# Last stage of a six-layer perceiver kernel: attention of all four tiles ahead of the ternary layers

## The chip, the cores and the metric

The kernel runs on one core of one Trainium2 chip, as one program. The metric is device microseconds of one execution of the whole program, lower is better. Before the change three executions took 3087.1, 3088.03 and 3089.5 us; the median is 3088.03 us.

## The reference

x holds 8 batches of 64 tokens of width 512, all float32. Six residual layers follow each other; the change lies in the last two, the fifth and sixth, which the kernel computes in one stage:

```python
x = x + _L1_attn_ref(_layernorm(x, axis=-1), Wq, Wk, Wv, u, v, Wo, bo)
x = x + _L1_ffn_ref(_layernorm(x, axis=-1), w1, b1, w2, b2)

# fifth: attention with relative positions, 16 heads of 32, per batch of 64 tokens
scores = (Q @ K.T + u @ K.T + rel_shift(Q @ r.T + v @ r.T)) / sqrt(32)
out = softmax(scores) @ V;  return out @ Wo + bo

# sixth: two ternary linear layers, 512 -> 2048 -> 512
def act_quant(x):                      # levels of -128 to 127 per token
    scale = 127.0 / clip(max(abs(x)), 1e-5)
    return clip(round(x * scale), -128, 127) / scale
def bitlinear(x, w, b):
    return act_quant(rmsnorm(x)) @ weight_quant(w).T + b     # weights of -1, 0, 1
h = gelu(bitlinear(x, w1, b1));  return bitlinear(h, w2, b2)
```

## The kernel before, in words

The 512 tokens are four tiles of 128 tokens (NT = 4, two batches in a tile); x stays in SBUF for the whole program. Five earlier stages run from 0 to about 2900 us of the span and are the same in both kernels. The last stage is `l1_tail` (L1938 to L2262). It works as follows.

- `Group(...).turn` (L1997) normalizes a group's tiles and transposes them (`xt_ps`, L2003); `queries` (L2012) projects them (`q_ps`, L2008) into qu and qv; `keys` (L2092, `k_ps`) and `values` (L2099, `v_ps` L2103) give kT and v. `first` holds tiles 0 to 2; `last` holds tile 3 alone, whose x comes last from the stage before.
- `positions_of(t)` (L2050) computes the relative-position scores `y_ps`, copies them to y and writes them to a DRAM buffer `shift` (L2056); `shifted(t)` (L2065) reads them back displaced as z (L2068). Both DMAs stand in SP's queue, together with the loads of weights (`w1q` L1912, `w2q` L1917) and of the wide biases b1 and b2 (L1971).
- `probabilities(t)` (L2109): sixteen score matmuls `s_ps` (L2041), addition of z (L2115), maximum (L2119), subtraction (L2120), Exp on ScalarE (L2121), sum, reciprocal and product (L2122 to L2124). Apart from the matmuls and the Exp this is on VectorE.
- `turn` (L2127) transposes p on TensorE (`pT_ps`, L2133) with copies on ScalarE (L2134); `attend` (L2137) multiplies by v (`o_ps`, L2146) and selects heads into oT (L2155 on ScalarE, L2156 on VectorE); `out` (L2161) is four matmuls with Wo (`out_ps`, L2164) and the addition to x (L2171).
- `hidden(t)` (L2183): statistics of x (L2188 to L2193), the level through `rms_levels` (L1920; its power of -1/2 is on GpSimd, L57), the rounding (L1933), the transposition `turn_levels` (`levels_ps` L2177, copy L2181), sixteen bf16 matmuls `h_ps` (L2204), then four times: bias and scale (L2208, VectorE), Gelu (L2209, ScalarE), Square with a sum (L2211, ScalarE), maximum (L2212, VectorE). It ends with the addition of b2 to x on GpSimd (L2213).
- `hidden_levels` (L2216) makes the second quantization of the 2048 hidden values; `layer2` (L2225) transposes them (L2177, copies L2179 and L2181), multiplies by w2 (`o_ps`, L2231), adds (L2233) and writes the tile out (L2234).

The code gives an order of calls, and the tile layer's scheduler then interleaves instructions of neighbouring calls on each engine; what each engine executes is the fixed order of the built program. Buffers also bind the order: the PSUM pool `pm` has three banks (tag "mm": s, pT, o, out, o2), `pe` three (tag "e": q, k, y, h), `pt` two (levels); the SBUF tag "ring" has three buffers for qv, p and pT, and "big" has three, which the weights Wq, Wk, Wv hold first and the hidden rows h of the tiles afterwards.

The order of calls before the change: keys, p(0), values, out(0); p(1); all projections of tile 3; then for each t: hidden(t), layer2(t-1), p(t+2), hidden_levels(t), out(t+2), with out(1) in place of layer2 in the first turn. So one tile's ternary layers lie between the attention of two others.

Of the kernel before, what the change touches and what calls it, by code (L numbers as in the profile page):

```python
# [22 lines left out]
NT = B * S // P  # L23
# [1914 lines left out]
def l1_tail(K, x, d, w, known):  # L1938
# [7 lines left out]
    FIRST = NT - 1  # L1946
    with ExitStack() as es:
        ep = es.enter_context(tc.tile_pool(name="e_e", bufs=1, reuse_waits="tile"))
        wp = es.enter_context(tc.tile_pool(name="e_w", bufs=1, reuse_waits="tile"))
# [3 lines left out]
        pm = es.enter_context(tc.tile_pool(name="e_psm", bufs=3, space=PSUM))  # L1953
# [12 lines left out]
        def bank(name):  # L1966
            return pe.tile([P, D], F32, tag="e", name=name)
# [20 lines left out]
        class Group:  # L1988
# [8 lines left out]
            def turn(self):  # L1997
                for i, t in enumerate(self.tiles):
                    xn = ep.tile([P, D], F32, tag="xn", name="xn")
                    K.normalizer(rp, x[:, t : t + 1, :], known[t] if t < FIRST else None)(0, xn)  # L2000
                    ps = bank("xt_ps")
                    for c in range(DC):
                        nc.tensor.transpose(ps[:, ts(c, P)], xn[:, ts(c, P)], K.ident)  # L2003
                    nc.scalar.copy(self.xT[:, :, ts(i, P)], ps.rearrange("p (c n) -> p c n", n=P))
# [45 lines left out]
        def positions_of(t, qv):  # L2050
            y = ep.tile([P, 2, DC, 2, S + 1], F32, tag="y", name="y", bufs=2)
            halves = of_pairs(pe, "e", qv, lambda r, c, b: rT[r], "y_ps")
            nc.gpsimd.memset(y[:, :, :, :, 0:1], 0.0)
            for j in range(2):
                K.copy(y[:, j, :, :, 1:], halves[j])
            nc.sync.dma_start(  # L2056
                shift[t].rearrange("g (p k) -> p g k", k=S + 1), y.rearrange("p j c b k -> p (j c b) k")
            )

        first = Group(ep, list(range(FIRST)))  # L2060
# [27 lines left out]
        groups = [first]  # L2088
# [3 lines left out]
        def keys(g, psum, tag):  # L2092
            n = len(g.tiles) * P
            for c in range(DC):
                ps = psum.tile([P, D], F32, tag=tag, name="k_ps")[:, :n]
                g.project(wk, c, ps)
                nc.scalar.copy(kT[:, c, ds(g.tiles[0] * P, n)], ps)

        def values(g, psum, tag):  # L2099
            for i, t in enumerate(g.tiles):  # L2100
                ps = psum.tile([P, D], F32, tag=tag, name="v_ps")
                for c in range(DC):
                    nc.tensor.matmul(  # L2103
                        ps, lhsT=g.xT[:, c, ts(i, P)], rhs=wv[:, c, :], start=c == 0, stop=c == DC - 1
                    )
                K.copy(v[:, t, :], ps)
                nc.gpsimd.tensor_add(x[:, t, :], x[:, t, :], bo)

        def probabilities(t):  # L2109

            p = ring("j", "p")
            qu = groups[t // FIRST].qu[:, :, t % FIRST]
            halves = of_pairs(pm, "mm", qu, lambda r, c, b: kT[r, c, ds((2 * t + b) * S, S)], "s_ps")
            for j in range(2):
                nc.vector.tensor_add(p[:, j], halves[j], z[t][:, j])  # L2115
            rows = p.rearrange("p j c b k -> p (j c b) k")
            m = rp.tile([P, 16], F32, tag="m", name="m")
            wide = m.unsqueeze(2).to_broadcast([P, 16, S])
            nc.vector.tensor_reduce(m, rows, AX.X, ALU.max)  # L2119
            nc.vector.tensor_sub(rows, rows, wide)  # L2120
            nc.scalar.activation(rows, rows, AF.Exp)  # L2121
            nc.vector.tensor_reduce(m, rows, AX.X, ALU.add)  # L2122
            nc.vector.reciprocal(m, m)
            nc.vector.tensor_mul(rows, rows, wide)  # L2124
            return p
# [11 lines left out]
        def attend(t, pT):  # L2137
            o = [
                pm.tile([P, D], F32, tag="mm", name="o_ps").rearrange("p (c h q) -> p c h q", c=DC, h=2)
                for _ in range(2)  # L2140
            ]
            for c in range(DC):
                for j in range(2):
                    for b in range(2):
                        r = ds(64 * b, 64)
                        nc.tensor.matmul(  # L2146
                            o[b][ds(64 * j, 64), c].rearrange("p h q -> p (h q)"),
                            lhsT=v[r, t, ds(c * P + 64 * j, 64)],
                            rhs=pT[r, j, c, :],
                            start=True,  # L2150
                            stop=True,
                        )
            oT = rp.tile([P, DC, 2, S], F32, tag="oT", name="oT")
            for b in range(2):
                nc.scalar.activation(oT[:, :, b, :], o[b][:, :, 0, :], AF.Copy, scale=own[:, 2:3])  # L2155
                nc.vector.scalar_tensor_tensor(  # L2156
                    oT[:, :, b, :], o[b][:, :, 1, :], own[:, 3:4], oT[:, :, b, :], ALU.mult, ALU.add
                )
            return oT

        def out(t, oT):  # L2161
            ps = pm.tile([P, D], F32, tag="mm", name="out_ps")
            for c in range(DC):
                nc.tensor.matmul(  # L2164
                    ps,
                    lhsT=oT[:, c].rearrange("p b q -> p (b q)"),
                    rhs=wo[:, c, :],
                    start=c == 0,
                    stop=c == DC - 1,
                )  # L2170
            nc.vector.tensor_add(x[:, t, :], x[:, t, :], ps)  # L2171
# [11 lines left out]
        def hidden(t):  # L2183
            y = rp.tile([P, D], F32, tag="y", name="y")
            st = rp.tile([P, 6], F32, tag="lt_st", name="lt_st")
            mv = rp.tile([P, 2], F32, tag="l1_mv", name="l1_mv")
            top = rp.tile([P, 1], F32, tag="top", name="top")
            nc.vector.bn_stats(st, x[:, t, :])  # L2188
            nc.vector.bn_aggr(mv, st)


            nc.vector.tensor_scalar(y, x[:, t, :], mv[:, 0:1], None, ALU.subtract)
            nc.vector.tensor_reduce(top, y, AX.X, ALU.max, apply_absolute_value=True)  # L2193
            level = rms_levels(K, rp, y, top, mv[:, 1:2], 1.0 + EPS, EPS * EPS)
            nc.vector.tensor_mul(level, level, w.size[:, 0:1])
            xT = rp.tile([P, DC, P], BF16, tag="xT", name="xT")
            turn_levels(y, xT, False)
            h = big("h")
            tops = rp.tile([P, 4], F32, tag="tops", name="tops")
            squares = rp.tile([P, 4], F32, tag="squares", name="squares")  # L2200
            for n in range(4):
                ps = bank("h_ps")
                for c in range(DC):
                    nc.tensor.matmul(  # L2204
                        ps, lhsT=xT[:, c, :], rhs=w.w1[:, c, ts(n, 512)], start=c == 0, stop=c == DC - 1
                    )
                hn = h[:, ts(n, 512)]
                nc.vector.scalar_tensor_tensor(hn, ps, level, b1[:, ts(n, 512)], ALU.mult, ALU.add)  # L2208
                nc.scalar.activation(hn, hn, AF.Gelu)  # L2209
                sq = rp.tile([P, D], F32, tag="sq", name="sq")  # L2210
                nc.scalar.activation(sq, hn, AF.Square, accum_out=squares[:, n : n + 1])  # L2211
                nc.vector.tensor_reduce(tops[:, n : n + 1], hn, AX.X, ALU.max, apply_absolute_value=True)  # L2212
            nc.gpsimd.tensor_add(x[:, t, :], x[:, t, :], b2)  # L2213
            return h, tops, squares
# [10 lines left out]
        def layer2(t, h, level):  # L2225
# [7 lines left out]
            nc.vector.scalar_tensor_tensor(o, ps, level, x[:, t, :], ALU.mult, ALU.add)  # L2233
            nc.sync.dma_start(d["out"][ts(t, P), :], o)  # L2234

        keys(first, pm, "mm")
        p = probabilities(0)
        values(first, pm, "mm")
        out(0, attend(0, turn(p)))
        p = probabilities(1)  # L2240
        last = Group(wp, [FIRST])
        last.turn()
        last.queries()
        keys(last, pe, "e")
        values(last, pe, "e")
        positions_of(FIRST, last.qv[0])
        groups.append(last)
        got = None
        for t in range(NT):
            h = hidden(t)  # L2250
            if t == 0:
                out(1, attend(1, turn(p)))
                shifted(FIRST)
            else:
                layer2(t - 1, *got)
            if t + 2 < NT:
                p = probabilities(t + 2)
            got = hidden_levels(*h)
            if t + 2 < NT:
                out(t + 2, attend(t + 2, turn(p)))  # L2260
        layer2(NT - 1, *got)


def program(tc, d):
# [137 lines left out]
```

## Time and profile before

| what | value |
|---|---|
| median of three runs | 3088.03 us |
| the profiled execution's own time | 3083.06 us |
| its span, first to last instruction | 3081.1 us |
| mean granted TensorE clock | 0.987 of full |
| PE, DVE, ACT, POOL busy over the span | 97%, 59%, 27%, 32% |
| from 2944 to 3078 us (134 us): PE, DVE, ACT, POOL busy | 102.3, 88.4, 51.3, 10.3 us |
| granted clock in that stretch | 0.90 |
| last VectorE instruction of the kernel ends (3077.36 + 0.75) | 3078.1 us |

PE is TensorE's matmuls, PEld its weight loads, DVE VectorE, ACT ScalarE, POOL GpSimd, SP the engine whose queue issues the DMAs. A tile is named by what an instruction writes and reads (`out_ps<-L1a_Wo,oT`), L2164 is the line of the kernel. A float32 matmul appears as two records in the profile (x8 for the four matmuls of `out`), a bf16 one as one.

### The profile page before, as it was taken

The page shows a single profiled execution, that of the slowest core. Times are in us where ns is not written, and L with a number is a line of the kernel's source. Part 1 is how long each engine was busy: PE and PEld are TensorE (multiplying, and loading weights), DVE is VectorE, ACT ScalarE, POOL GpSimd, SP SyncE. Part 2 cuts the span into 40 slices and gives each one's busy share as a digit, 9 for nine tenths or more (in the row PEclk, how much of TensorE's full clock was granted, in tenths as well). Part 3 has the DMA queues.
Part 4 walks back from the last instruction along what each step waited for, and adds up shares of the span by engine and source line. Part 5 has one row for each costly group of instructions (what it writes and reads, how often), then busy time and mean ns, then how long its engine had stood idle before and what let it go on. Part 6 is the DMA issues. An engine that isn't in the chain of part 4 may idle for free.

```text
span 3081.1 us, 41104 instructions
## 1 busy us (share of the span) xinstructions
PE 2980.5 (97%) x15515; PEld 2288.4 (74%) x15521; DVE 1830.5 (59%) x3124; ACT 845.5 (27%) x1620; POOL 993.0 (32%) x959
## 2 busy tenths in 40 slices
PE   8999999999999989999999999999999999999887
PEld 7777778888888767888654446778788888888654
DVE  4845545666656656666433333578676676676746
ACT  2322241222222322222111222232332333323234
POOL 4434343544454534444110003221422413304000
PEclk9999999999999999999999999999999999999998
DMA  8265474434434564432659974302112022020260
GB/s 263 71 200 152 145 244 128 140 100 143 131 103 132 180 188 134 128 119 66 228 185 339 343 253 144 92 15 75 42 51 77 21 73 58 22 89 3 87 107 14
DMA packets 387187, 391.76 MB, mean 127 GB/s; under 512 B 55054, under 2 KB 289558, under 8 KB 385838
## 3 DMA queue, kind: packets, MB, share of 16 engines
q1 hardware_dynamic: 380761, 371.80, 39.2%
q10 hardware_dynamic: 5589, 15.24, 1.3%
q8 instruction: 123, 2.02, 0.3%
q0 software_dynamic: 640, 2.10, 0.2%
q14 instruction: 74, 0.61, 0.1%
HBM read 332.90 MB, written 56.16 MB: 126 GB/s over the span
## 4 chain that ended last, share of the span: by engine, by line
PE 58%; DVE 2%; ACT 1%; DMA 1%; issue 0%; POOL 0%; POOLq 0%; ACTq 0%; DVEq 0%; SPq 0%
PE x_ps L1528 11%; PE y_ps L1528 8%; PE s_ps L1691 6%; PE oe_ps L1231 4%; PE h_ps L1204 4%; PE acc L1742 3%; PE x_ps L585 3%; PE x_ps L468 2%; PE z_ps L585 2%; PE z_ps L468 1%; PE sum_ps L1575 1%; PE y_ps L585 1%; PE y_ps L468 1%; DMA wo<-in_L1x_Wp 1%; PE vt_ps L1619 1%; PE top_ps L1727 1%
## 5 line engine op out<-in xcount | busy, mean ns | idle before, releaser
L1588 POOL TENSOR_TENSOR r<-r,minus_half 128x52 f32<-128x52 f32 x32 | 276.9, 8673 | 558.0 <-DVE r L1587 558.0
L468 PE MATMUL x_ps<-qt,ctxT 128*128 128x256 f32 x1152 | 288.1, 384 | 9.6 <-ACT u L428 6.9
L585 PE MATMUL x_ps<-pt,ctx 128*128 128x256 f32 x1152 | 281.7, 382 | 7.2 <-DVE a L561 6.3
L468 PEld LDWEIGHTS x_ps<-qt,ctxT 128*128 128x128 f32 x1152 | 218.7, 192 | 50.4 <-ACT u L428 8.8
L585 PEld LDWEIGHTS x_ps<-pt,ctx 128*128 128x128 f32 x1152 | 217.3, 190 | 41.1 <-DVE a L561 6.5
L136 POOL TENSOR_TENSOR ctxT<-ctxT 128x256 f32<-128x256 f32 x96 | 79.0, 823 | 412.4 <-DMA ctxT<-in_ctxT 284.5
L1691 PE MATMUL s_ps<-qb,kT 128*128 128x256 f32 x832 | 201.2, 381 | 0.1
L449 DVE TENSOR_TENSOR m<-m,s 128x512 f32<-128x512 f32 x176 | 137.5, 781 | 95.8 <-ACT s L447 93.2
L136 POOL TENSOR_TENSOR ctx<-ctx 128x256 f32<-128x256 f32 x96 | 73.5, 765 | 348.5 <-DMA ctx<-in_ctx 275.4
L1691 PEld LDWEIGHTS s_ps<-qb,kT 128*128 128x128 f32 x832 | 154.2, 190 | 26.2 <-issue 3.5
L501 DVE TENSOR_TENSOR s<-s,top_ps 128x1024 f32<-128x1024 f32 (+1 forms) x112 | 123.2, 1135 | 23.3 <-PE top_ps L491 23.3
L1733 DVE TENSOR_TENSOR s<-s,top_ps 128x1792 f32<-128x1792 f32 x64 | 117.9, 1884 | 28.8 <-PE top_ps L1727 28.8
L433 DVE SCALAR_TENSOR_TENSOR s<-y_ps,bias,p 128x256 f32<-128x256 f32 x96 | 46.3, 483 | 146.2 <-PE y_ps L468 145.8
L1701 DVE TENSOR_TENSOR s<-s_ps,r 128x512 f32<-128x512 f32 x192 | 126.4, 682 | 10.8 <-PE s_ps L1691 10.2
L1734 ACT ACTIVATE s<-s 128x1792 f32<-128x1792 f32 x64 | 101.0, 1591 | 84.0 <-DVE s L1733 84.0
L1742 PEld LDWEIGHTS acc<-s,v 128*64 128x64 f32 x1664 | 96.1, 138 | 32.4 <-issue 27.0
L502 ACT ACTIVATE s<-s 128x1024 f32<-128x1024 f32 (+1 forms) x112 | 110.8, 996 | 30.0 <-DVE s L501 25.9
L1742 PE MATMUL acc<-s,v 128*64 128x128 f32 x1664 | 114.9, 280 | 4.1 <-ACT s L1734 4.1
L1204 PE MATMUL h_ps<-w,tok 128*128 128x512 f32 x256 | 117.3, 593 | 0.0
L1231 PE MATMUL oe_ps<-w,hT 128*128 128x512 f32 x256 | 115.6, 593 | 0.0
L515 DVE TENSOR_TENSOR total<-total,s 128x512 f32<-128x512 f32 x160 | 110.0, 687 | 3.5
L468 PE MATMUL x_ps<-qk,ctxT 128*128 128x256 f32 x384 | 104.9, 391 | 6.2 <-ACT s L447 4.0
(472 smaller groups left out, 6287.2 us busy)
## 6 DMA issues: line engine op xcount, KB each, us to landing
w<-in_L0f_W SPq DMA_DIRECT2D x64, 1024.0 KB, 5.8
ctxT<-in_ctxT SPq DMA_DIRECT2D x240, 256.0 KB, 4.7
ctx<-in_ctx SPq DMA_DIRECT2D x192, 256.0 KB, 3.4
kept<-ctxT SPq DMA_DIRECT2D x48, 384.0 KB, 2.8
ctxT<-kept SPq DMA_DIRECT2D x48, 384.0 KB
wvT<-in_L0x_WvT SPq DMA_DIRECT2D x16, 1024.0 KB, 8.4
qk<-qk_all SPq DMA_DIRECT2D x15, 1024.0 KB, 7.4
qk_all<-stage SPq DMA_DIRECT2D x32, 384.0 KB, 3.5
```

Source lines behind the costliest of these rows:

```text
L136: nc.gpsimd.tensor_add(q[:, 4, :], q[:, 2, :], q[:, 3, :])
L449: nc.vector.tensor_max(self.m, self.m if k else self.s[:, LAST, :], self.s[:, k, :])
L468: nc.tensor.matmul(ps, lhsT=ctxT[i][:, Quarters.LEFT[n], ts(e, P)], rhs=right[n][:, e, :], start=start and e == 0, stop=e == 1, skip_group ...
L501: nc.vector.tensor_sub(s[:, k : k + n], s[:, k : k + n], top.unsqueeze(1).to_broadcast([P, n, HALF]))
L585: nc.tensor.matmul(ps, lhsT=ctx[pair][:, Quarters.LEFT[n], ts(m, P)], rhs=right[n][:, i, :], start=start and i == 0, stop=i == 2, skip_gro ...
L1204: nc.tensor.matmul(ps, lhsT=self.tok[:, c, :], rhs=self.w1[n][:, c, :], start=c == 0, stop=c == DC - 1)
L1231: nc.tensor.matmul(ps, lhsT=self.hT[:, f, :], rhs=self.w2[f // 4][:, f % 4, :], start=f == 0, stop=f == 15)
L1528: nc.tensor.matmul(ps, lhsT=left(n, e), rhs=right(n, e), start=start and e == 0, stop=e == 1, skip_group_check=not start,)
L1588: nc.gpsimd.tensor_tensor(r, r, minus_half, ALU.pow)
L1691: nc.tensor.matmul(ps[:, i].rearrange("p h q -> p (h q)"), lhsT=kT[c][:, ts(k0 + i, P)], rhs=qb[c].rearrange("p h q -> p (h q)"), start=Tr ...
L1701: nc.vector.tensor_mul(out, ps, by)
L1742: nc.tensor.matmul(acc[ds(64 * j, 64), c, :], lhsT=v[:, k, ds(c * P + 64 * j, 64)], rhs=s[:, k, ts(j, P)], start=k == 0, stop=k == NK - 1,)
```

## The change

Only the list of calls at the end of `l1_tail` changes; the functions, tiles, pools and loads are the same. All four tiles' softmax and output come first, with the projections of tile 3 placed between `turn(p(0))` and `out(0)`; the ternary layers follow, where hidden(t+1) is called before hidden_levels(t) and layer2(t).

```diff
+        last = Group(wp, [FIRST])
+        groups.append(last)
         keys(first, pm, "mm")
-        p = probabilities(0)
-        values(first, pm, "mm")
-        out(0, attend(0, turn(p)))
-        p = probabilities(1)
-        last = Group(wp, [FIRST])
+        turned = turn(probabilities(0))
         last.turn()
         last.queries()
+        positions_of(FIRST, last.qv[0])
+        values(first, pm, "mm")
         keys(last, pe, "e")
+        shifted(FIRST)
+        out(0, attend(0, turned))
+        turned = turn(probabilities(1))
         values(last, pe, "e")
-        positions_of(FIRST, last.qv[0])
-        groups.append(last)
-        got = None
+        p = probabilities(2)
+        out(1, attend(1, turned))
+        turned = turn(p)
+        p = probabilities(3)
+        out(2, attend(2, turned))
+        turned = turn(p)
+        h = hidden(0)
+        out(3, attend(3, turned))
         for t in range(NT):
-            h = hidden(t)
-            if t == 0:
-                out(1, attend(1, turn(p)))
-                shifted(FIRST)
-            else:
-                layer2(t - 1, *got)
-            if t + 2 < NT:
-                p = probabilities(t + 2)
-            got = hidden_levels(*h)
-            if t + 2 < NT:
-                out(t + 2, attend(t + 2, turn(p)))
-        layer2(NT - 1, *got)
+            ahead = hidden(t + 1) if t + 1 < NT else None
+            layer2(t, *hidden_levels(*h))
+            h = ahead
```

In the built program the number of TensorE, VectorE, GpSimd and SP instructions is the same in both kernels, apart from bare waits; ScalarE has two loads of a function table fewer (12 for 14). The order is the same up to the first score matmuls of tile 0 (`s_ps`, L2041).

## The prediction, made before the changed kernel ran

> **What bounds the kernel now.** First the page: both orders are the same up to 2943.6 us, so only the last 134 us can change. Then the busy time by stretches (columns: PE, PEld, DVE, ACT, POOL busy us, granted clock, DMA share, GB/s):
>
> ```profile
> span 3081.1 us, 41104 instructions
> ...
> 2944.00:2986.00 42.00, 37.29 (x243) 23.47 (x242) 24.70 (x43) 14.86 (x30) 1.82 (x2) 1.00 0.68 137
> 2986.00:3023.00 37.00, 24.62 (x153) 14.28 (x153) 24.52 (x56) 16.13 (x33) 3.83 (x4) 0.77 0.09 16
> 3023.00:3060.00 37.00, 26.39 (x162) 15.28 (x164) 28.21 (x66) 12.91 (x23) 4.10 (x5) 0.91 0.04 15
> 3060.00:3078.00 18.00, 13.97 (x70) 7.88 (x69) 10.93 (x25) 7.39 (x16) 0.55 (x1) 0.91 0.04 15
> ```
>
> See: up to 2986 PE is nearly full; after that no engine is (PE 65 of 92 us, VectorE 64), and the clock falls. It is a stage of waits, one engine for another. VectorE's timeline gives its milestones: L2171 is where a tile's attention is added to x, L2208 where its hidden layer reaches the Gelu.
>
> ```profile
> 2962.25 0.69 DVE L2171 TENSOR_TENSOR x<-x,out_ps 128x512 f32<-128x512 f32 x1 [4.02 <-PE out_ps L2164]
> ...
> 2983.03 3.34 DVE L2208 SCALAR_TENSOR_TENSOR h<-h_ps,rl_level,b 128x512 f32<-128x512 f32 x4 [1.79 <-PE h_ps L2204]
> ...
> 2999.79 0.69 DVE L2171 TENSOR_TENSOR x<-x,out_ps 128x512 f32<-128x512 f32 x1 [6.78 <-PE out_ps L2164]
> ...
> 3011.82 0.74 DVE L2208 SCALAR_TENSOR_TENSOR h<-h_ps,rl_level,b 128x512 f32<-128x512 f32 x1
> ...
> 3033.74 0.74 DVE L2208 SCALAR_TENSOR_TENSOR h<-h_ps,rl_level,b 128x512 f32<-128x512 f32 x1
> ...
> 3051.94 0.69 DVE L2171 TENSOR_TENSOR x<-x,out_ps 128x512 f32<-128x512 f32 x1 [3.79 <-PE out_ps L2164]
> ...
> 3059.73 1.61 DVE L2208 SCALAR_TENSOR_TENSOR h<-h_ps,rl_level,b 128x512 f32<-128x512 f32 x2 [0.69 <-PE h_ps L2204]
> ...
> 3077.36 0.75 DVE L2233 SCALAR_TENSOR_TENSOR o<-o_ps,rl_level,x 128x512 f32<-128x512 f32 x1 [4.06 <-PE o_ps L2231]
> ```
>
> So the old stage is 2983.0 + 28.8 + 21.9 + 26.0 + 18.4 = 3078.1: one rhythm per tile, in which the next tile's whole attention stands between two hidden layers, then the last tile alone. The chain of waits shows what a cold PE costs; out(1) and out(3) are the same four matmuls:
>
> ```profile
> 2993.06 6.70 PE out_ps L2164 x8
> ...
> 3048.20 3.71 PE out_ps L2164 x8
> ```
>
> **What the Trainium skill says.** "TensorE: Matmul & The Clock Gate", Part 1 (The HAM clock gate): PE runs at half rate after an idle window of about 3.4 us and at full rate after a busy one, the windows free-running. The trace agrees: the clock is 0.50 at 2988.9-2999.1, 3005.9-3012.8, 3040.1-3046.9, 3070.8-3074.2, each preceded by a stretch of 3.41 us with PE busy 32% or less (51% kept full clock); it came back after stretches busy 84% or more (77% did not do). "ScalarE: Activation LUTs", What ACT_TABLE_LOAD costs: 1283 ns a load and some 1380 ns of drain. The trace has 1283 ns and shows no drain (2982.40 starts 0.05 us after the work before it):
>
> ```profile
> L2209 ACT ACT_TABLE_LOAD x3 | 3.8, 1283 | 0.1
> ...
> L2121 ACT ACT_TABLE_LOAD x2 | 2.6, 1283 | 0.0
> ```
>
> The first page's Architectural detail has ScalarE and VectorE as strict FIFOs: what stands behind a wait waits. VectorE's timeline shows the program's order throughout.
>
> **The walk.** I lay the new order of each engine out by arithmetic: an instruction starts when the one ahead of it is through and what it needs has ended, at the durations above and in the same timelines. The same arithmetic on the old order, with the half-clock rule just read, finds all four cold stretches (one 3.4 us too long) and ends at 3080.2, measured 3078.1; without any half clock it ends at 3070.4.
>
> *Front, until out(0) is added: later by 15.6.* Old: the 12 values matmuls (10.5 us) hide p(0). New: behind `s_ps` PE holds `xt_ps` and 12 of 16 `q_ps` (0.6 + 3.0), then `pT` waits for p(0), whose VectorE and ScalarE chain is 1.3 + 1.2 + 1.2 + 1.1 + 1.2 + 0.25 + 1.2 us; with hand-overs it ends at 2951.0, PE idle 3.5. Then pT 1.0, values 14 x 0.87 = 12.2, q 1.0, a wait for a bank of q 1.3 (the qu, qv copies L2025, L2020), y 2.0, keys of tile 3 4.0, o 1.6, out 3.5: 2977.6, added at 2977.9 against 2962.3. Most of this is work that the old order did later.
>
> *First hidden layer: later by 12.5.* From 2977.9: addition and statistics with p(1)'s L2115, L2119, L2120 between them and the power on GpSimd, y rounded at 2985.3 (PE idle 4.0); levels, copy, first h_ps at 2986.7. Then pT(1), s(2), o(1) stand ahead of the rest of h_ps, and on VectorE p(2)'s first half ahead of L2208: 2995.5, old 2983.0.
>
> *First rhythm, three outs in it: 28.0, old 28.8.* out(1) is added at 3000.1. VectorE next has L2171 0.6, three L2212 1.8, L2208 with a wait 1.3, p(3)'s L2115 1.2, L2212 0.6, L2119 1.1, L2156 0.4, L2120 1.1 and the second L2156: 8.0, so out(2) starts at 3008.1 (PE idle 3.4), + 3.5 + p(3)'s last three 2.5 = 3014.1. Then pT(3) 1.1, copies 0.7, o 1.6, L2155 and L2156 with tile 0's rounding ahead 1.9, out(3) 3.5: added at 3022.9 against 3051.9. Tile 1's L2208 follows at 3023.5.
>
> *Two rhythms without attention: 13.5 and 11.0, old 21.9 and 26.0.* One tile's L2208 to its last sum is 3059.7 to 3066.6 = 6.9 (Gelu and Square on ScalarE set it); small operations, the power on GpSimd and the old tile's L2233 2.4; four L1933 1.6; the next L2208 stands right behind: 10.9. In the first, tile 2's statistics (1.9) and the b2 addition on GpSimd ahead of the power (L2213, 1.27, partly hidden) come in: 13.5. The hidden matmuls (3.6) and layer2's (3.6 + 2.2 transposes) hide under ScalarE's 6.9; were they cold, about 3 us a tile would show.
>
> *Last tile: 16.8, old 18.4.* Same chain; 1.6 of the old is the half clock at 3070.8-3074.2.
>
> Sum: 2995.5 + 28.0 + 13.5 + 11.0 + 16.8 = 3064.8 at full clock.
>
> *Table loads:* five become three, 2 x 1.28; only the one at 3035.9-3039.6 lay on the old chain (2.6 with its partner). Already inside the rhythms; the new ones lie where ScalarE waits (cost 0; 1 if they meet the Gelu).
>
> *Moved DMAs:* shift(3) and z(3) stand last in SP's queue but for the outputs in both orders, and now want to go earlier. b2 in front of them:
>
> ```profile
> 2959.54 0.64 SPq L1971 DMA_DIRECT2D b<-in_L1f_b  x1
> 2981.39 0.37 SPq L2056 DMA_DIRECT2D shift<-y  x1
> 2989.12 1.29 SPq L2068 DMA_DIRECT2D z<-shift  x2
> ```
>
> y(3) is copied at 2961, write 7.7 (2981.39 to 2989.12), two issues 1.3, landing 10.1 (the page's median): 2980. p(3)'s L2115 needs it at 3003.2: 23 us of cover, cost 0. With these four DMAs 30 us slower in sum, 4.
>
> *Half clock:* the new order has three idle stretches (3.5, 4.0, 3.4 us), and how they fall on the 3.41-us grid sets how many go cold. Lower end 0: dense work hides it. Upper end: each followed by two half windows, 3 x 1.7 = 5. I take 1.5. The other way, the old order lost 3080.2 - 3070.4, about 8 to 10.
>
> 3064.8 + 1.5 = 3066.3. Against 3078.1 measured that is 11.8; against the same walk of the old order (3080.2) 13.9. I take 13. The profiled execution would go from 3083.06 to 3070; it lies 5 below the median, nothing shows that the 5 depends on this stage, so the median goes 3088.03 - 13.0 = **3075.0**.
>
> **Rivals.** 0.2% (6.2 us) is about what a measurement can tell.
> 1. *As walked*, 70%: 3075, own range 3070.5 to 3079.5.
> 2. *The idle is only half moved: cold PE as expensive as before*, 12%. Both at full clock: 3070.4 - 3064.7 = 5.7 gain, 3082.3. For it: three idle stretches, as many as before's costly ones. Against: they are followed by long dense matmuls, and the ternary rhythms have none.
> 3. *Better*, 14%: VectorE's queue has slack the walk rounds away; 64 us of its work after 2986 in the old order against 79 us walked; 18 gained, 3070.
> 4. *Slower: half clock settles in the front*, 4%. PE idles 2947.6-2951.0, so the window after it is cold; if no stretch then passes 84% busy until 3000 (bank waits, bursts of 16 small matmuls), the walk ends at 3086.0, 21 later: 3086.0 - 3078.1 = 7.9, 3095.9. It decides at 2957: eleven values matmuls in a row, 9.5 us, should fill a window; against it speaks that.
> The change not doing what it says is out: the built order shows it.
>
> **Range and chances.** 3069 to 3081.5: case 1, two thirds of case 3, a sixth of case 2, some 81%. Faster by over 0.2%: cases 1, 3, a quarter of 2, 87%. Same: the rest of 2, 9%. Slower: 4%.
>
> **What would show it.** Right: L2171 at about 2978, 3000, 3014, 3023; L2208's rhythms near 28, 13.5, 11; three table loads; z(3) never waited for; after 3023 full clock. Wrong: clock 0.5 through 2957-3000; L2171 of out(3) after 3032; a rhythm without attention above 16; VectorE waiting for z.

## The result and the profile after

| | before | changed |
|---|---|---|
| median of 10 runs each | 3087.45 us (3078.35 to 3089.71) | 3079.41 us (3074.66 to 3082.64) |
| ratio | | 0.9973, 95% interval 0.9965 to 0.9981 |
| on a second chip, 34 and 6 runs | 3083.45 us | 3073.65 us, ratio 0.9970 (0.9958 to 0.9982) |
| profiled execution | 3083.06 us | 3074.66 us |
| first `s_ps` of tile 0 to the end of the last L2233 | 136.48 us | 128.19 us; on the second chip 127.13 us |

The kernel is faster by 8 us (9 to 10 on the second chip), where 13 were forecast. The last row is the measure used below, "the stage". Up to its first instant all the kernels here execute the same instructions, and yet their profiled executions reach that instant between 2937.5 and 2948.5 us. A difference of a few us between two whole programs is therefore read from the stage, and a whole median only where its interval is clear of the other. The stage is not exact either: it comes from one execution of each kernel, and the same new front took from 36.9 to 41.1 us in the seven executions below that have it unchanged.

The first line of the changed kernel's page, and then its busy time in the same stretches as before (PE, PEld, DVE, ACT, POOL, granted clock, DMA share, GB/s):

```profile
span 3072.2 us, 41098 instructions
```

```profile
2944.00:2986.00 42.00, 33.82 (x208) 22.09 (x208) 18.77 (x32) 9.70 (x22) 2.81 (x2) 0.96 0.75 149
2986.00:3023.00 37.00, 30.29 (x227) 19.64 (x230) 30.06 (x62) 17.34 (x32) 3.73 (x4) 0.82 0.00 1
3023.00:3060.00 37.00, 29.33 (x144) 15.44 (x146) 32.08 (x82) 20.53 (x45) 3.75 (x6) 1.00 0.04 15
3060.00:3078.00 18.00, 7.56 (x42) 4.11 (x40) 5.03 (x13) 1.38 (x2) 0.19 (x1) 0.90 0.08 30
```

The third row is what the change gives: VectorE 32 of 37 us busy, full clock, the rhythm of the ternary layers without attention in it. The first row is what it takes: TensorE is busy for 33.8 of 42 us, where it was busy for 37.3 before. VectorE's timeline has the milestones (L2171 adds a tile's attention, L2208 starts its hidden layer, L2233 is the last sum):

```profile
2978.91 0.69 DVE L2171 TENSOR_TENSOR x<-x,out_ps 128x512 f32<-128x512 f32 x1 [4.02 <-PE out_ps L2164]
...
2998.71 0.74 DVE L2208 SCALAR_TENSOR_TENSOR h<-h_ps,rl_level,b 128x512 f32<-128x512 f32 x1
...
3003.18 0.68 DVE L2171 TENSOR_TENSOR x<-x,out_ps 128x512 f32<-128x512 f32 x1
...
3018.13 0.68 DVE L2171 TENSOR_TENSOR x<-x,out_ps 128x512 f32<-128x512 f32 x1
...
3027.96 0.69 DVE L2171 TENSOR_TENSOR x<-x,out_ps 128x512 f32<-128x512 f32 x1 [0.33 <-PE out_ps L2164]
3028.57 1.44 DVE L2208 SCALAR_TENSOR_TENSOR h<-h_ps,rl_level,b 128x512 f32<-128x512 f32 x2
...
3041.91 1.40 DVE L2208 SCALAR_TENSOR_TENSOR h<-h_ps,rl_level,b 128x512 f32<-128x512 f32 x2
...
3052.68 0.75 DVE L2208 SCALAR_TENSOR_TENSOR h<-h_ps,rl_level,b 128x512 f32<-128x512 f32 x1
...
3068.49 0.75 DVE L2233 SCALAR_TENSOR_TENSOR o<-o_ps,rl_level,x 128x512 f32<-128x512 f32 x1 [3.20 <-PE o_ps L2231]
```

The chain of waits still holds cold work, that is, work at half clock: `pT` of tile 0 at 1.97 us for 1.04. out(1) is at full clock (3.70, before 6.70); and the table loads of the stage are three:

```profile
2951.75 1.97 PE pT_ps L2133 x8
...
2998.85 3.70 PE out_ps L2164 x8
```

```profile
L2209 ACT ACT_TABLE_LOAD x2 | 2.6, 1283 | 0.0
L2121 ACT ACT_TABLE_LOAD x1 | 1.3, 1283 | 0.0
```

### The profile page after: what moved, and what is told of

Its sections match the earlier page's. It is cut to its first block, busy times and chain, and to the rows that moved or that the text cites. A ratio compares the mean times of both kernels' runs of the same rounds, so it can differ in the third digit from the quotient of the medians.

```text
span 3072.2 us, 41098 instructions
## 1 busy us (share of the span) xinstructions
PE 2979.5 (97%) x15516; PEld 2287.8 (74%) x15521; DVE 1827.7 (59%) x3124; ACT 843.2 (27%) x1618; POOL 993.9 (32%) x959
## 4 chain that ended last, share of the span: by engine, by line
PE 57%; DVE 3%; DMA 2%; ACT 1%; issue 0%; POOL 0%; SPq 0%; POOLq 0%; ACTq 0%; DVEq 0%
PE x_ps L1528 11%; PE y_ps L1528 8%; PE s_ps L1691 6%; PE h_ps L1204 4%; PE oe_ps L1231 4%; PE acc L1742 4%; PE x_ps L585 3%; PE x_ps L468 2%; PE z_ps L585 2%; PE z_ps L468 1%; PE sum_ps L1575 1%; PE y_ps L585 1%; PE y_ps L468 1%; DMA wo<-in_L1x_Wp 1%; PE vt_ps L1619 1%; PE top_ps L1727 1%
## 5 line engine op out<-in xcount | busy, mean ns | idle before, releaser
L501 DVE TENSOR_TENSOR s<-s,top_ps 128x1024 f32<-128x1024 f32 (+1 forms) x112 | 123.2, 1135 | 22.9 <-PE top_ps L491 22.9
L1733 DVE TENSOR_TENSOR s<-s,top_ps 128x1792 f32<-128x1792 f32 x64 | 117.9, 1884 | 28.8 <-PE top_ps L1727 28.8
L1701 DVE TENSOR_TENSOR s<-s_ps,r 128x512 f32<-128x512 f32 x192 | 126.5, 682 | 10.8 <-PE s_ps L1691 10.2
L1742 PEld LDWEIGHTS acc<-s,v 128*64 128x64 f32 x1664 | 97.0, 139 | 32.4 <-issue 27.0
```

The source lines that it names most:

```text
L501: nc.vector.tensor_sub(s[:, k : k + n], s[:, k : k + n], top.unsqueeze(1).to_broadcast([P, n, HALF]))
L1701: nc.vector.tensor_mul(out, ps, by)
L1742: nc.tensor.matmul(acc[ds(64 * j, 64), c, :], lhsT=v[:, k, ds(c * P + 64 * j, 64)], rhs=s[:, k, ts(j, P)], start=k == 0, stop=k == NK - 1,)
```

## The experiments

All milestones in one table, in us after the first `s_ps` of tile 0, from one profiled execution each. "Walk" is the prediction's own layout of the new order, at full clock. out(t) is the instant at which the attention of tile t is added to x (L2171), and L2208 is the start of a hidden layer.

| kernel | out(0) | L2208, tile 0 | out(1) | out(2) | out(3) | L2208, tile 3 | end |
|---|---|---|---|---|---|---|---|
| before | 20.6 | 41.4 | 58.2 | 83.2 | 110.3 | 118.1 | 136.5 |
| walk | 36.3 | 53.9 | 58.5 | 72.5 | 81.3 | 106.4 | 123.2 |
| changed | 37.9 | 57.7 | 62.1 | 77.1 | 86.9 | 111.6 | 128.2 |
| e5 changed again | 36.9 | 56.6 | 61.1 | 76.0 | 85.9 | 110.6 | 127.1 |
| e1 new front, old rest | 36.9 | 48.8 | 65.4 | 90.0 | 117.0 | 124.8 | 144.7 |
| e2 old front, new rest | 20.6 | 45.9 | 50.0 | 63.4 | 73.3 | 96.0 | 114.1 |
| e3 sequential ternary | 38.7 | 58.1 | 62.5 | 77.0 | 85.8 | 131.5 | 148.1 |
| e4 before, no tables | 20.6 | 42.4 | 55.5 | 76.7 | 107.4 | 115.2 | 133.7 |
| e6 changed, filler before out(2) | 36.9 | 56.4 | 60.9 | 75.8 | 85.9 | 110.6 | 127.2 |
| e7 before, filler before o(1) | 20.6 | 40.8 | 56.3 | 80.7 | 110.1 | 117.9 | 136.5 |
| e8 values cover p(0) | 32.4 | 51.4 | 55.9 | 70.8 | 80.7 | 105.4 | 121.9 |
| e9 no b2 addition | 41.1 | 60.5 | 65.0 | 79.4 | 88.2 | 112.6 | 130.6 |
| e10 e8 and e9 | 32.4 | 51.3 | 55.8 | 70.2 | 79.0 | 103.4 | 121.4 |
| e11 e6 and e9 | 39.2 | 60.8 | 65.3 | 79.6 | 89.3 | 113.7 | 131.6 |

### Which half of the change gains: e1 and e2

The change has two parts, the front (everything up to out(0), with tile 3's projections in it) and the rest. e1 has the new front and the old loop, e2 the old front and the new rest:

e1, against the changed kernel:

```diff
-        turned = turn(probabilities(1))
+        p = probabilities(1)
         values(last, pe, "e")
-        p = probabilities(2)
...
+        got = None
         for t in range(NT):
-            ahead = hidden(t + 1) if t + 1 < NT else None
-            layer2(t, *hidden_levels(*h))
-            h = ahead
+            h = hidden(t)
+            if t == 0:
+                out(1, attend(1, turn(p)))
+            else:
+                layer2(t - 1, *got)
...
```

The loop is that of before without its `shifted(FIRST)`. e2, against the kernel before, has the changed kernel's list of calls from `turned = turn(p)` on:

```diff
         positions_of(FIRST, last.qv[0])
         groups.append(last)
-        got = None
-        for t in range(NT):
...
+        shifted(FIRST)
+        turned = turn(p)
+        p = probabilities(2)
+        out(1, attend(1, turned))
+        turned = turn(p)
...
+            ahead = hidden(t + 1) if t + 1 < NT else None
+            layer2(t, *hidden_levels(*h))
+            h = ahead
```

> The new front (projections of tile 3 between the transposition of p(0) and out(0)) with the old loop behind it, everything computed. My theory: the front alone is a loss, because the values matmuls no longer hide p(0); the walk puts out(0) at 2978 and the end 5 us later than before: slower than before by 3 to 7 us. Rival (having tile 3's projections done early is what frees the later rhythms): as fast as before or faster, by 0 to 8 us.

> The old front (values under p(0), out(0), then p(1) and tile 3's projections) with the new rest: attention of tiles 1 to 3 first, ternary layers in a pipeline of two. Everything is computed. My theory: out(0) at 2962 again and the whole gain of the rest: 14 to 19 us faster than before, about 6 faster than the changed kernel (3073 where that is 3079). Rival (the new front is needed for the gain): 8 us faster than before or less.

| | old rest | new rest |
|---|---|---|
| old front | 1 | 0.9934 (0.9921 to 0.9946), 3059.2 us |
| new front | 1.0039 (1.0027 to 1.0051), 3093.21 us | 0.9973 (0.9965 to 0.9981) |

By the medians the new front costs 0.39%, 12 us, and the new rest gains 0.66%, 20 us. The table alone would say that the parts simply add, but its intervals reach 2 to 4 us to either side, and the stage says otherwise. There the front costs 8.2 us with the old rest (136.5 to 144.7) and 13.0 to 14.1 with the new one (114.1 to 127.1 and 128.2); the new rest gains 22.4 us with the old front and 16.5 to 17.6 with the new one. With the old rest the first L2208 is only 7.4 us later, with the new one 10.7 to 11.8. What makes this difference was not separated.

The signs are the same in both measures. e1 was slower by more than either theory gave it, e2 faster by a little more. So e2 beats both kernels by far, and the change gives up 12 us or so of its own gain for its front. TensorE's timeline shows why. e2 between out(0) and the first hidden layer:

```profile
2962.41 2.72 PE L2008 MATMUL q_ps<-xT,L1a_Wq 128*128 128x128 f32 x22
2967.65 1.13 PE L2008 MATMUL q_ps<-xT,L1a_Wq 128*128 128x128 f32 x8 [2.52 <-DVE qu L2025]
...
2972.81 3.60 PE L2103 MATMUL v_ps<-L1a_Wv,xT 128*128 128x512 f32 x8
2976.34 2.00 PE L2041 MATMUL y_ps<-c_rT,qv 64*128 64x64 f32 x32
2978.27 1.09 PE L2133 MATMUL pT_ps<-ident,p 128*128 128x128 f32 x8
2979.30 2.37 PE L2041 MATMUL s_ps<-kT,qu 64*128 64x64 f32 x32
2981.60 1.74 PE L2146 MATMUL o_ps<-pT,v 64*64 64x128 f32 x32
2983.27 0.66 PE L2177 MATMUL levels_ps<-ident,y 128*128 128x128 f32 x4
```

and the changed kernel between `xt_ps` and the same place:

```profile
2951.75 1.97 PE L2133 MATMUL pT_ps<-ident,p 128*128 128x128 f32 x8 [4.50 <-DVE p L2124]
...
2980.66 1.98 PE L2103 MATMUL v_ps<-L1a_Wv,xT 128*128 128x512 f32 x4
2986.93 1.11 PE L2177 MATMUL levels_ps<-ident,y 128*128 128x128 f32 x4 [4.28 <-DVE y L1933]
2988.82 1.46 PE L2204 MATMUL h_ps<-w1q,xT 128*128 128x512 bf16 x3 [0.78 <-ACT xT L2181]
2990.07 1.91 PE L2133 MATMUL pT_ps<-ident,p 128*128 128x128 f32 x8
2991.91 2.39 PE L2041 MATMUL s_ps<-kT,qu 64*128 64x64 f32 x32
```

Tile 3's projections are work that needs nobody. In e2 they fill the time in which VectorE makes p(1) and the first rounded y, and `levels_ps` starts without a wait. In the changed kernel they are already done: TensorE waits 4.50 us for p(0), 4.28 us for y, and is cold behind both. In both kernels the work is the same; what was lost is its cover, the time of another engine that it used to fill. Half clock goes with it: in the stage, e2 has one cold stretch of 3.4 us, the changed kernel 17 us in three, and the kernel before 27 us in four.

### The values as cover of p(0): e8 (and e5, the changed kernel beside it)

```diff
-        turned = turn(probabilities(0))
+        p = probabilities(0)
+        values(first, pm, "mm")
+        turned = turn(p)
...
-        values(first, pm, "mm")
```

> The changed kernel once more, on the chip of the next three kernels, so that each can be set against it. Theory: 0.9973 of the kernel before again, 8 us faster. If the half clock falls elsewhere from chip to chip, the time moves by up to the 5 us that the prediction gave it at most; the cold stretches at 2986.0 to 2992.8 and 3009.8 to 3016.6 then lie elsewhere.

> The changed kernel with one call moved: the value matmuls of tiles 0 to 2 stand between p(0) and its transposition again, as in the kernel before, instead of behind tile 3's positions. Theory (the new front costs because p(0) has lost its cover): the 4.5 us in which TensorE waited for p(0) go, and so does the cold stretch behind it; the kernel is 4 to 7 us faster than the changed kernel. Rival (the front costs because tile 3's projections and keys stand ahead of out(0), whatever covers p(0)): the wait turns up at the next place, out(0) comes at the same time to 1 us, and the time is within 1.5 us of the changed kernel.

```profile
2946.66 10.57 PE L2103 MATMUL v_ps<-L1a_Wv,xT 128*128 128x512 f32 x24
2957.06 1.04 PE L2133 MATMUL pT_ps<-ident,p 128*128 128x128 f32 x8
2957.94 0.60 PE L2003 MATMUL xt_ps<-ident,xn 128*128 128x128 f32 x4
```

There is no wait before `pT`, which runs at full clock. out(0) is added 4.5 us sooner than in e5, and the stage is 5.2 us shorter than e5's, 6.3 than the first profile's. In the stage that is what the theory said, and the 4.28 us wait for y stays, as it must. e10, which has the same front, also adds out(0) at 32.4 us, and none of the seven executions without the cover is below 36.9. In the whole program the gain cannot be told from noise (3071.43 against 3073.65 us on the same chip, intervals 0.9954 to 0.9979 and 0.9958 to 0.9982): e8's profiled execution reached the stage at 2944.7, e5's at 2942.2. The remaining 7.8 us to e2 are the other half of the front: e2 differs from e8 in where tile 3's projections and `turn(p(1))` stand. These two were not moved one at a time. e5 itself repeats the first result, and its cold stretches lie where they lay: behind the waits for p(0), for y and for oT of out(2).

### The pipeline of two tiles: e3

```diff
-            ahead = hidden(t + 1) if t + 1 < NT else None
             layer2(t, *hidden_levels(*h))
-            h = ahead
+            h = hidden(t + 1) if t + 1 < NT else None
```

> The changed kernel, but hidden(t+1) is called after layer2(t), so the ternary layers have no pipeline. Everything is computed. My theory: attention done as early as in the changed kernel (about 3028), but rhythms of 18 to 19 us a tile in place of 13 and 11: slower than the changed kernel by 18 to 22 us, slower than before by 8 to 13. Rival (the gain is in the attention of all tiles standing together): within 5 us of the changed kernel.

3097.6 us, ratio 1.0047 (1.0034 to 1.006): 0.74%, 23 us, above the changed kernel; in the stage 20 to 21. The rhythms, from one tile's first L2208 to the next tile's, are 19.7 and 20.1 us in place of 13.3 and 10.8, and in each the rounding leaves TensorE standing, then cold:

```profile
3058.80 3.63 PE L2204 MATMUL h_ps<-w1q,xT 128*128 128x512 bf16 x16 [0.78 <-ACT xT L2181]
3069.25 1.94 PE L2177 MATMUL levels_ps<-ident,h 128*128 128x128 f32 x8 [6.82 <-DVE h L1933]
```

This is the expected size, and the rival (it is enough that the attention of all tiles stands together) falls: without hidden(t+1) ahead of layer2(t) the stage is even 3.4 us longer than e1's, which has the same front and the old rest. The whole gain of the rest hangs on that pipeline.

### Table loads: e4

```diff
-                nc.scalar.activation(hn, hn, AF.Gelu)
+                nc.scalar.activation(hn, hn, AF.Square)
```

The edit is in the kernel before. With it no table is changed in the stage, and the Gelu is not computed.

> The kernel before with a square in place of the Gelu: that one function isn't computed; all activations then use one table and the five loads are gone. The prediction's theory (loads cost what lies on the chain, 2.6 us, the rest hidden): faster than before by 1 to 4 us. Rival (the loads, and the order that they force on ScalarE and through it on VectorE, are what the change really saves): faster by 8 to 12 us, as fast as the changed kernel. The built order on VectorE differs too, so a result near 10 speaks for loads and order together.

The result is 3080.57 us, ratio 0.9992 (0.9984 to 1.0), and the stage is 2.8 us shorter. TensorE spends 27 us of the stage at half clock in both kernels, so that is not what differs. The loads, together with the order on VectorE that changes with them, are worth two or three us, not eight.

### Half clock: e6 and e7

Float32 matmuls (`warm`, with the identity as weights) whose result is overwritten were put where TensorE stood still; nothing else moves. e6 has three of them in the changed kernel, on the bank of out(2); e7 has four in the kernel before, on a bank of o(1). The list at the end gives their number for each tile:

```diff
+        warm = lambda ps, rhs, n: [nc.tensor.matmul(ps, lhsT=K.ident, rhs=rhs, start=True, stop=True) for _ in range(n)]
...
+            ps = pm.tile([P, D], F32, tag="mm", name="out_ps"); pT is not None and warm(ps, pT[:, 1].rearrange("p c n -> p (c n)"), [0, 0, 3, 0][t])
...
+            ]; warm(o[0].rearrange("p c h q -> p (c h q)"), pT[:, 0].rearrange("p c n -> p (c n)"), [0, 4, 0, 0][t])
```

> The changed kernel with three more float32 matmuls (their results are overwritten), put in the bank of out(2) just before its four matmuls, where TensorE waited 3.14 us for oT at half-clock cost; the order of everything else is the same. Theory (half clock took what is missing of the forecast): the stretch at 3009.8 to 3016.6 stays at full clock, out(2) takes 3.6 instead of 5.9 us, h_ps behind it no longer lags, and the kernel is 2 to 3 us faster than the changed kernel. Rival (VectorE and ScalarE set the first rhythm, the clock is a bystander): out(2) is shorter, the hidden layer of tile 1 comes at the same time, and the time is within 1 us of the changed kernel.

> The kernel before with four more float32 matmuls (their results are overwritten) just before o_ps of tile 1, where TensorE stood still before the long cold stretch of 2988.9 to 2999.1; the order of everything else is the same. Theory: the stretch goes or shrinks, out(1) takes 3.6 instead of 6.7 us, and the kernel is 2 to 4 us faster than before. Rival (a cold stretch that is removed only moves to the next wait): the time is within 1 us of before and another stretch is cold for longer.

Both rivals hold. In e6 the clock stays full up to out(2), which falls from 5.91 to 3.70 us, but what follows is not sooner:

```profile
3011.74 2.84 PE L2126 MATMUL out_ps<-pT,ident 128*128 128x512 f32 x6
3014.95 3.70 PE L2164 MATMUL out_ps<-L1a_Wo,oT 128*128 128x512 f32 x8 [0.37 <-DVE oT L2156]
3021.15 1.06 PE L2133 MATMUL pT_ps<-ident,p 128*128 128x128 f32 x8 [2.50 <-DVE p L2124]
...
3023.48 1.97 PE L2146 MATMUL o_ps<-pT,v 64*64 64x128 f32 x28
```

`pT` of tile 3 waits for VectorE's p(3), and out(2) is added 14.96 us after out(1), against 14.95 in the changed kernel. Those 2.2 us of half clock cost nothing. But the clock is not full behind them: a cold stretch of 3.4 us now lies on the next matmuls, `o_ps` of tile 3 (the last line, 1.97 us where the changed kernel took 1.09), and out(3) follows out(2) by 10.1 us instead of 9.8. In e7 out(1) is added 1.9 us sooner, but out(3) then meets a cold stretch of its own, and the stage is as long as before:

```profile
3041.42 6.14 PE L2164 MATMUL out_ps<-L1a_Wo,oT 128*128 128x512 f32 x8 [1.47 <-DVE oT L2156]
```

In the kernel before these four matmuls took 3.70. The half clock of the stage is 27 us in both. A cold stretch taken away at one place may come back at the next wait.

### VectorE and GpSimd: e9, e10, e11

What else could hold the first rhythm? GpSimd and VectorE in the changed kernel:

```profile
2984.11 1.54 POOL L57 TENSOR_TENSOR rl_rms<-l_mv,nhalf 128x1 f32<-128x1 f32 x1 [1.70 <-DVE l_mv L56]
3013.52 1.26 POOL L2213 TENSOR_TENSOR x<-x,b 128x512 f32<-128x512 f32 x1 [27.87 <-DVE l_mv L56]
...
3020.86 1.44 POOL L2213 TENSOR_TENSOR x<-x,b 128x512 f32<-128x512 f32 x1 [5.05 <-DVE y L2192]
```

```profile
3015.33 0.21 DVE L1929 TENSOR_SCALAR top<-top,rl_rms 128x1 f32<-128x1 f32 x1 [1.10 <-POOL rl_rms L57]
3015.46 1.21 DVE L2122 TENSOR_REDUCE m<-p 128x16 f32<-128x1024 f32 x1
...
3020.70 2.69 DVE L1933 TENSOR_SCALAR h<-h,rl_scale 128x512 f32<-128x512 f32 x4
```

The b2 addition stands ahead of the power in GpSimd's queue, and p(3)'s last three operations stand behind the wait for that power in VectorE's. And the four roundings take 2.69 us where the same four take 1.66 to 1.68 in each of its later tiles, just while the next addition runs. The Trainium skill describes such a lock: "SBUF — State Buffer", section "SBUF: two separate sides", says that the port pair which the two engines share is "an exclusive lock, not a bandwidth split": a GpSimd operation and a VectorE operation with two SBUF inputs, or in a mode that uses both ports, exclude each other for a whole instruction. The trace agrees: one of the four roundings, from 3021.09, takes 1.50 us instead of 0.48 and ends 0.3 us after the addition, and the power at 2984.11 takes 1.54 instead of 0.55 beside VectorE's L2120, which has two SBUF inputs (2984.01 to 2985.24; no run takes that one away). Which of the two kinds of VectorE operation the rounding is, the trace does not say.

```diff
-            nc.gpsimd.tensor_add(x[:, t, :], x[:, t, :], b2)
```

> The changed kernel without the addition of b2 to x on GpSimd (L2213; b2 is left out of the sixth layer's output, everything else is computed); the order on TensorE, VectorE and ScalarE is the same. Theory (part of what is missing of the forecast is VectorE waiting for GpSimd): tile 1's L1929, with p(3)'s last three operations queued behind it, no longer waits 1.1 us for a power that stands behind the addition; the rounding of tile 0's hidden levels takes 1.67 us again instead of 2.68, since no addition runs beside it; from the first scores of tile 0 to the last sum the stage is 2 to 3 us shorter than the changed kernel's 127.1 to 128.2. Rival (the whole of it is half clock): those two places change, the waits turn up at TensorE, and the stage is within 0.7 us of the changed kernel's.

> Both edits together: the value matmuls of tiles 0 to 2 stand between p(0) and its transposition, and b2 is not added (b2 is left out of the output). Theory: the two costs lie at different places of the chain and add up: the stage is 7 to 9 us shorter than the changed kernel's 127.1 to 128.2, so about 119 to 120 us. Rival (one hides the other): 121 to 122 us, as with the first edit alone.

> The three filler matmuls before out(2) and no addition of b2 (b2 is left out of the output), together. Either edit alone left the other chain to set the instant at which out(2) is added: with the filler alone it was p(3) on VectorE (14.96 us after out(1), no gain), without b2 alone it was a cold out(2) (14.42 us, VectorE waited 0.44 us for it). Theory (two chains of nearly the same length meet there): with both, out(2) is added 13.8 to 14.0 us after out(1). Rival (the 0.44 us were another wait): 14.4 us again.

e9's whole stage, 130.6 us, is longer than the changed kernel's: the expectation missed. The table says where. Its out(0) came 3.3 us later than the changed kernel's, before the edit has any effect (z(0) landed 1.9 us after the scores, and the clock was half for some 10 us of the front). L1929 no longer waits. From out(0) to out(3) it took 47.1 us against 49.0 (48.9 in e5): out(1) to out(2) 14.4 for 14.95, out(2) to out(3) 8.8 for 9.8, the roundings at their old length. In the last tile 1.4 us of that are gone again: `o_ps` of tile 2 runs cold, 5.30 us where the changed kernel's order took 3.62, and VectorE waits for it. Whether this loss belongs to the edit is open: all three kernels without the addition (e9, e10, e11) are cold there, the first profile, e5, e6 and e8 are not, and e2, which has the addition, is. From out(0) to the end, 0.8 to 0.9 us of the gain are left.

```profile
3023.52 1.67 DVE L1933 TENSOR_SCALAR h<-h,rl_scale 128x512 f32<-128x512 f32 x4
...
3065.34 0.75 DVE L2233 SCALAR_TENSOR_TENSOR o<-o_ps,rl_level,x 128x512 f32<-128x512 f32 x1 [1.32 <-PE o_ps L2231]
```

e10 shows both again: against e8, out(3) is 1.6 us sooner, so at that place the two costs add, and the end only 0.6 us sooner, after the same cold `o_ps`; its 121.4 us are the rival's number, reached in another way. In whole medians none of it shows (0.9966 and 0.9959, with intervals that overlap those of e5 and e8).

In e9 out(2) had become the later of two chains:

```profile
3020.95 0.69 DVE L2171 TENSOR_TENSOR x<-x,out_ps 128x512 f32<-128x512 f32 x1 [0.44 <-PE out_ps L2164]
```

e11 takes both away. That wait is gone, but out(2) came 14.3 us after out(1), between the theory's 13.8 to 14.0 and the rival's 14.4: the scores of tile 3 were 0.4 us later, behind a stretch at half clock that in this execution lasted until 3008. By its number e11 is inconclusive; what it adds is the range of the half clock. With the same order of instructions, out(0) to the first L2208 took 21.7 us here, cold for some 14 us, 19.4 to 19.8 in e5, e6, e9 and the first profile, cold for some 7, and 18.9 to 19.0 in e8 and e10, cold for some 3.5.

## Why the prediction was right, and by what it was off

The direction, the mechanism and most of the steps were right. The size was not: 8 us came of the 13, and the median, 3079.41, lies at the very end of what the prediction gave its own case (3070.5 to 3079.5).

- *Two rhythms without attention, 13.5 and 11.0, and the last tile, 16.8*: measured 13.3, 10.8, 16.6. e3 shows that it is the pipeline that makes them.
- *Table loads*: three, and on no chain; e4 puts the worth of all five of the old order at two to three us.
- *Moved DMAs, cost 0*: z(3) was issued at 2971.95. The write took 11.9 us (2960.03 to 2971.95), not 7.7, and the cover of 23 us was wide enough: p(3)'s L2115 waited for its scores (0.88 us), not for z.
- *After 3023 full clock*: so in the changed kernel's profile, up to the last sum.

```profile
2960.03 0.37 SPq L2056 DMA_DIRECT2D shift<-y  x1
2971.95 1.30 SPq L2068 DMA_DIRECT2D z<-shift  x2
```

```profile
3007.18 1.29 DVE L2115 TENSOR_TENSOR p<-s_ps,z 128x512 f32<-128x512 f32 x2 [0.88 <-PE s_ps L2041]
```

The walk was off by five us: the stage took 128.2 where the walk had 123.2, and the forecast had set 1.5 aside for half clock. By the terms of the sum, for the first profile:

| step of the prediction | predicted | measured | what it was |
|---|---|---|---|
| out(0) | 36.3 | 37.9 | z(0) landed 0.9 us after the scores, on the path since p(0) has no cover (e5, without that: 36.9); the other 0.7 is put down to the half clock behind that wait |
| out(0) to first L2208 | 17.6 | 19.8 | cold levels, `pT` and scores (1.11, 1.91, 2.39 us for 0.66, 1.05, 2.00), 1.7; the power locked out, 0.5 |
| out(1) to out(2) | 14.0 | 14.95 | VectorE's own sum up to out(2)'s start: the L2208 with its wait took 1.6, not 1.3, and the second L2156 (0.4) was named but not added: the prediction's operations make 8.5, not 8.0 |
| out(2) to out(3) | 8.8 | 9.8 | the rounding beside the b2 addition; 8.8 in e9, 8.8 in e10 |
| rest | 46.5 | 45.8 | smaller terms, L2208 to out(1) and the three tiles behind out(3) |

The wait of p(0) for z, in the first profile and in e5:

```profile
2944.01 1.29 DVE L2115 TENSOR_TENSOR p<-s_ps,z 128x512 f32<-128x512 f32 x2 [7.41 <-DMA z<-shift]
```

```profile
2944.24 1.29 DVE L2115 TENSOR_TENSOR p<-s_ps,z 128x512 f32<-128x512 f32 x2 [6.80 <-PE s_ps L2041]
```

So *"Half clock: ... I take 1.5"* was too small, at 2.4 us on the path, and it was not alone. Another 2.4 us are VectorE's: 0.95 are its queue, half of it a slip in the prediction's sum, and 1.5 are the port shared with GpSimd, which a walk made of single durations could not contain. 0.9 us are a DMA that the old order covered.

One term was right by luck. From the start of out(2) the prediction added out(2)'s 3.5 us and p(3)'s last three operations, 6.0 in all. Measured were 6.0 from the end of the second L2156 to L2171, but on another path: VectorE's statistics of tile 1, the wait of 1.1 us for GpSimd's power, then p(3)'s last three. out(2)'s own length is not in it, as e6 shows.

The half clock at out(2), which I would have blamed from the trace alone, costs nothing (e6). Rival 2, cold TensorE as dear as before, is half right: three stretches stayed, and of them only the one behind p(0) and most of the one behind y were on the path. Rival 4's mechanism, half clock that settles in the front, was seen in part in e9 and e11, where out(0) came 1 to 4 us later than in the changed kernel's two profiles (a part of this is z(0), which landed 1.9 us after the scores in e9 and 1.1 in e11); nothing like 21.

What the prediction did not ask is whether the front was needed. It wrote of it "Most of this is work that the old order did later", and did not see that where it stood this work covered p(1) and the first y. The old front with the new rest gains 20 us (e2), more than twice what the change gains.

Three things stay open. How much of the front's 12 us is idle and how much the half clock behind it was not separated: fillers before the first `levels_ps` change the order of what follows and were not run. Why the front costs 8 us with the old rest and 13 to 14 with the new one is not known. And why the cold stretches fall differently from execution to execution is not shown.

## What to carry to other kernels

Before moving work forward, ask what it covers where it stands: here independent matmuls were worth most behind the longest chains of the other engines, and done early they left those chains bare, and TensorE cold behind them. A pipeline of two tiles pays by the other tile's work standing ahead of the wait. Cut a change into its parts and run each: a large gain and a large loss together look like one small gain. Price a stall by removing it: in e6 and e9 a second chain of nearly the same length stood right behind.

## What the runs showed of the hardware

- Executions of the same instructions differ, and the clock is part of it. Entry into the stage went from 2937.5 us (e7) to 2948.5 (e3) with the same instructions ahead of it; by windows of 10 us the two had about 48 and 61 us at half clock before it. 14 us more at half clock account for at most 7 of these 11 us, by an estimate that takes TensorE as busy throughout, and the changed kernel and e8, with 51 us each, entered 3.7 us apart. The rest is not explained.
- GpSimd and VectorE held each other up in stretches as short as one instruction: 0.48 us became 1.50 (0.48 again without the addition, e9), 0.55 became 1.54.
- A TensorE that waits 1.8 us and then runs small transpositions went cold in some executions and not in others with the same order on TensorE from out(0) on (`o_ps` of tile 2, 3.62 in e8, 5.30 in e9 and e10; these two lack the addition on GpSimd).
